# Moving the sums of the 32-wide score squares to TensorE, and more of the scores to GpSimd

## The chip, the cores and the metric

The kernel runs on one core of one Trainium2 chip. The metric is the device time of one execution in microseconds; lower is better. A core has five instruction streams that matter here: PE (TensorE; its weight loads are listed apart as PEld), DVE (VectorE), ACT (ScalarE), POOL (GpSimd) and SP, which issues DMAs. Each stream runs its own instructions in order and waits for the others through semaphores.

## The reference

The input x is (8, 512, 256): 8 batches of 512 tokens of width 256. Four blocks follow one another, each on a layer norm of x and each added to x: attention A, a feed-forward block, attention B, and the same feed-forward block again.

```python
# attention A: per token, the 64 channels of a head attend to one another
Q, K, V = (x @ W + b).reshape(b, s, 16, 64)            # Q scaled by 64**-0.5
scores = einsum('bshq,bshk->bshqk', Q, K)               # outer product, 64x64 per token and head
scores = where(triu(ones((64, 64)), 1), -inf, scores)   # causal in the channels
attn = einsum('bshqk,bshk->bshq', softmax(scores), V)
x = x + attn.reshape(b, s, 1024) @ Wo + bo
# feed-forward: 256 -> 1024 (gated, silu) -> 1024 (gelu) -> 1024 (gelu) -> 256, ternary weights
# attention B: the usual causal attention over 512 tokens, 16 heads of width 16
```

Attention A has no matrix product in its middle: for every token and head it needs a triangle of exp(q_i k_j), its row sums (the denominator), and its row sums weighted with v_j (the numerator).

## The kernel before

**Groups and units.** Attention A works on groups (batch b, four heads g, token tile i): 8 x 4 x 4 = 128 groups of 128 tokens by 256 channels. The triangle of a head is cut into squares below the diagonal: one of 32, two of 16, four of 8 and so on down to 1, and the diagonal itself. `units` splits a group into NU = 4 units: unit 0 holds the squares of 32 of two heads, unit 1 the squares of 16 of all four heads, unit 2 the squares of 32 of the other two heads, unit 3 all the smaller ones. Units 0 to 2 have 2048 score elements per token each, unit 3 has 1920. A tile `w` of 4096 columns holds the exponentials and, beside them, the exponentials times v.

**One unit's way.** `scores` multiplies q by k (POOL for units 0 and 2, DVE for units 1 and 3). `exps` takes the exponential on ACT. `weigh` multiplies by v on DVE. `halve` starts a DMA on POOL's queue that adds the second half of `w` to the first (units 0 to 2). For the squares of 32 `fold` then adds the halves of what is left on POOL. `gather` reduces the rest over the last axis on DVE into a small tile `red`, and `add_rows` adds that on POOL to `acc`, which holds denominator and numerator of the group. For unit 3 `gather` does the squares of 8 and 4, and `small_squares` those of 2 and 1 on POOL. When all units are in, `invert` (DVE) and `divide` (POOL) finish the group, `turn_group` transposes it on PE, and `project_out` multiplies it by Wo.

**The order.** It is written out by hand. `AttentionA.step(n)` issues the work of one step, one unit per step; `self.at(n - k)` is the unit that is k steps old, so the stages of different units overlap. A step has three parts, ended by `yield`. With u = n mod 4 for the unit that enters at step n, the parts always meet the same stages: `project` (q, k, v on PE) stands in part 2 of steps with n mod 4 = 1, `keep_qk` (ACT copies q and k out of PSUM) and `turn_group` in part 2 of n mod 4 = 2, `project_out` in part 2 of n mod 4 = 3, `new_x` in part 2 of n mod 4 = 0. After each part the main loop inserts slices of the rest (`after_a`: feed-forward, attention B, feed-forward of the previous batch), as much as a running total of estimated costs allows (`total = 309.5` per batch). So attention A of batch b runs beside the other three blocks of batch b - 1; batch 0 of attention A runs nearly alone, and so do the last three blocks of batch 7.

**Buffers.** The `w` tiles of units 0 and 2 rotate through three buffers; unit 1 has one of its own (`w16`). In PSUM there are two `qv` tiles (q and v of a group), five tiles `ps_f` for the other blocks, and `bank`, one tile of two halves of 256 columns; `half_bank` hands its halves out in turn to `project` (k), `turn_group`, `project_out` and the transpose of a layer norm of attention A.

Of the kernel before, what the change touches and what calls it, by code (L numbers as in the profile page):

```python
# [9 lines left out]
F32 = mybir.dt.float32  # L10
# [6 lines left out]
P = 128  # L17
# [267 lines left out]
def fast_path(ctx: ExitStack, tc: tile.TileContext, k, t, flag):  # L285
# [214 lines left out]


    bank = ps_a.tile([P, 2, GW], F32, name="bank")
    halves = [0]

    def half_bank():
        halves[0] ^= 1
        return bank[:, halves[0], :]

    def judge():

# [72 lines left out]

    JB = 8

    def pieces(w, n, off, nsq, cols):

        def of_rows(v):
            return v[:, cols].rearrange("p (x t) -> p x t", t=2 * n)[:, :, n:]

        def of_cols(v):
            return v[:, cols].rearrange("p (x t) -> p x t", t=2 * n)[:, :, :n]

        if n < 16:
            e, ev = (
                w[:, a * SMALL + off : a * SMALL + off + nsq * n * n].rearrange("p (x i j) -> p x i j", i=n, j=n)  # L600
                for a in range(2)
            )
            yield e, ev, lambda v: of_rows(v).unsqueeze(3), lambda v: of_cols(v).unsqueeze(2)
            return
        both = w.rearrange("p (b a x i j) -> p a b x i j", a=2, x=nsq, i=n, j=JB)
        if n == 32:
            for x in range(nsq):
                yield (
                    both[:, 0, :, x],
                    both[:, 1, :, x],  # L610
                    lambda v, x=x: of_rows(v)[:, x].unsqueeze(1).unsqueeze(3),
                    lambda v, x=x: of_cols(v)[:, x].rearrange("p (b j) -> p b j", j=JB).unsqueeze(2),
                )
        else:
            for k in range(n // JB):
                yield (
                    both[:, 0, k],
                    both[:, 1, k],
                    lambda v: of_rows(v).unsqueeze(3),
                    lambda v, k=k: of_cols(v)[:, :, k * JB : (k + 1) * JB].unsqueeze(2),  # L620
                )

    class AttentionA:
# [33 lines left out]
        def step(self, n):  # L657

            weighed = self.at(n - 2)
            if weighed[0] is not None:  # L660
                self.weigh(*weighed)
            unit = self.at(n)
            on_pool = unit[3] in (0, 2)
            if on_pool:
                half = self.scores(*unit)
                next(half)
            if weighed[0] is not None:
                self.halve(*weighed)
            if on_pool:
                next(half, None)  # L670
            b, i, g, u = self.at(n + 40)
            if u == 0 and g == 0 and i == 0 and b > 0:
                self.x[b] = load_x(b)
            b, i, g, u = self.at(n + 10)
            if u == 0 and g == 0 and i == 0 and b > 0:
                self.measure(b)
            b, i, g, u = self.at(n + 8)
            if u == 0 and g == 0:
                self.live["xn"] = normed(self.x[b][:, i, :], *self.rn[b, i], "a")
            b, i, g, u = self.at(n - 5)  # L680
            if u == NU - 1:
                self.invert(b, i, g)
            b, i, g, u = self.at(n - 4)
            if u == 1:
                self.gather(b, i, g, u)
            b, i, g, u = self.at(n + 7)
            if u == 0 and g == 0:
                nc.scalar.copy(self.live[b, i], self.live.pop("ps_ln"))
            if self.at(n - 1)[0] is not None:
                self.exps(*self.at(n - 1))  # L690
            yield
            if unit[0] is not None and not on_pool:
                for _ in self.scores(*unit):
                    pass
            for args in self.sums:
                self.add_rows(*args)
            self.sums = []
            b, i, g, u = self.at(n - 5)
            if u == NU - 1:
                self.divide(b, i, g)  # L700
            b, i, g, u = self.at(n - 2)
            if u == NU - 1:
                self.small_squares(b, i, g)

            b, i, g, u = self.at(n - 4)
            if u == 0:
                self.fold(b, i, g, u)
            b, i, g, u = self.at(n - 3)
            if u == 2:
                self.fold(b, i, g, u)  # L710
            b, i, g, u = self.at(n - 9)
            if u == NU - 1:
                self.new_x(b, i, g)
            b, i, g, u = self.at(n + 2)
            if u == 0:
                self.keep_qk(b, i, g)
            b, i, g, u = self.at(n - 7)
            if u == NU - 1:
                self.turn_group(b, i, g)
            b, i, g, u = self.at(n - 8)  # L720
            if u == NU - 1:
                self.project_out(b, i, g)
            b, i, g, u = self.at(n + 3)
            if u == 0:
                self.project(b, i, g)
            yield
            b, i, g, u = self.at(n - 4)
            if u == 2:
                self.gather(b, i, g, u)
            b, i, g, u = self.at(n - 5)  # L730
            if u == 0:
                self.gather(b, i, g, u)
            b, i, g, u = self.at(n - 3)
            if u == NU - 1:
                self.gather(b, i, g, u)
            b, i, g, u = self.at(n - 7)
            if u == NU - 1:
                nc.scalar.copy(self.live["att"], self.live.pop("pta"))
            b, i, g, u = self.at(n + 8)
            if u == 0 and g == 0:  # L740
                self.live[b, i] = lnp.tile([P, DC, P], F32, tag="xnt_a", name=f"xnta_{b}_{i}", bufs=NT)
                self.live["ps_ln"] = turned_over(self.live.pop("xn"), half_bank().rearrange("p (c s) -> p c s", c=DC))
            yield

        def measure(self, b, tiles=range(NT)):
# [39 lines left out]
        def scores(self, b, i, g, n_u):  # L785

            qv, kt = self.live[b, i, g][:2]
            if n_u == 0:
                acc = ap_.tile([P, 2, GW], F32, tag="acc", name=f"acc_{b}_{i}_{g}", bufs=3)
                self.live[b, i, g].append(acc)  # L790
                nc.vector.tensor_tensor(acc[:, 0, :], qv[:, 0], kt[:, 0], ALU.mult)

            if n_u in (0, 2):
                w = wt.tile([P, 4096], F32, tag="w", name=f"w_{b}_{i}_{g}_{n_u}", bufs=3)
            elif n_u == 1:
                w = wt.tile([P, 4096], F32, tag="w16", name=f"w16_{b}_{i}_{g}")
            else:
                w = wt.tile([P, 2 * SMALL], F32, tag="ws", name=f"ws_{b}_{i}_{g}")
            self.live[b, i, g, n_u] = w
            eng, q = (nc.gpsimd, kt[:, 1]) if n_u in (0, 2) else (nc.vector, qv[:, 0])  # L800
            for n, off, nsq, cols in squares(units[n_u]):
                for e, ev, rows, columns in pieces(w, n, off, nsq, cols):
                    shape = list(e.shape)
                    eng.tensor_tensor(  # L804
                        e, rows(q).to_broadcast(shape), columns(kt[:, 0]).to_broadcast(shape), ALU.mult
                    )
                    yield

        def exps(self, b, i, g, n_u):
            w = self.live[b, i, g, n_u]  # L810
            if n_u == 0:
                acc = self.live[b, i, g][2]
                nc.scalar.activation(acc[:, 0, :], acc[:, 0, :], AF.Exp, scale=C**-0.5)
            if n_u < NU - 1:
                e = w.rearrange("p (b a r) -> p a b r", a=2, b=units[n_u][0][0] // JB)[:, 0]
            else:
                e = w[:, :SMALL]
# [15 lines left out]
                w = self.live[b, i, g, n_u]  # L833
                nc.gpsimd.dma_start(w[:, :2048], w[:, 2048:], accum_op=ALU.add)  # L834

        def fold(self, b, i, g, n_u):

            w = self.live[b, i, g, n_u]
            nc.gpsimd.tensor_tensor(w[:, :1024], w[:, :1024], w[:, 1024:2048], ALU.add)  # L839

        def columns_of(self, w, n, off, nsq):

# [4 lines left out]

        def small_squares(self, b, i, g):

            w = self.live[b, i, g, NU - 1]  # L850
            for n, off, nsq, cols in squares(units[NU - 1]):
                if n <= 2:
                    both = self.columns_of(w, n, off, nsq)
# [4 lines left out]
        def gather(self, b, i, g, n_u):  # L858


            w = self.live.pop((b, i, g, n_u))
            for n, off, nsq, cols in squares(units[n_u]):
                if n > 2:
                    red = ap_.tile([P, 2, nsq * n], F32, tag=f"red{nsq * n}", name=f"red_{b}_{i}_{g}_{n_u}_{n}", bufs=2 + (n < 32))
                    nc.vector.tensor_reduce(red, self.columns_of(w, n, off, nsq), AX.X, ALU.add)  # L865
                    self.sums.append((b, i, g, n, cols, red))

# [158 lines left out]

    def fits(i, w, src):

        both = wt.tile([P, 2 * HB], F32, tag="w", name=f"w32_{i}", bufs=3)
        nc.sync.dma_start(both[:, :HB], src)  # L1030
        nc.vector.tensor_tensor(both[:, HB:], both[:, :HB], w, ALU.not_equal)
        nc.vector.tensor_reduce(unfit[:, i : i + 1], both[:, HB:], AX.X, ALU.max)
# [439 lines left out]
```

## Time and profile before

| | |
|---|---|
| Timed runs | 3984.17, 3989.1 and 3989.51 us; median 3989.1 us |
| Profiled execution, first to last instruction | span 3990.8 us; no other time is listed for it, and the span lies 0.04% above the median of the timed runs |
| Busy | PE 3039.9, PEld 2055.2, DVE 3375.9, ACT 2341.3, POOL 3077.9 us |
| Mean granted clock of TensorE | 0.849 |
| DMA queue on POOL (q0) | 570.46 MB, its packets took 63.2% of the 16 DMA engines' time |

"Busy" counts the time in which an engine executes an instruction; issuing DMAs and waiting on semaphores is not counted. A group line gives source line, engine, operation, output and inputs with their shapes, the count, then busy microseconds and the mean nanoseconds of one, then the idle time ahead of it and who ended it. `w<-w` DMA lines are the accumulating transfers of `halve`.

### The profile page before, as it was taken

Reading aid. Unit: us, or ns where it says so; the run is one execution under the profiler, and the core shown is the slowest. Engines: PE = TensorE matmul, PEld = TensorE weight load, DVE = VectorE, ACT = ScalarE, POOL = GpSimd, SP = SyncE. Lnnn points to the kernel's source line nnn. Section 1 sums busy time; section 2 is a strip of 40 time slices with the busy share of each in tenths; the row PEclk is TensorE's granted clock in tenths of the full one; section 3 lists DMA queues with packets and bytes.
Section 4 is the critical chain, followed back from the end, with each engine's and each line's share of the span. In section 5 each row is a group of like instructions: output and inputs, shape, how many; then the busy total and the mean of one; then the engine's idle time right before and its main releaser. Section 6 shows DMA issues by size and latency. Waiting matters only on the chain.

```text
span 3990.8 us, 37932 instructions
## 1 busy us (share of the span) xinstructions
PE 3039.9 (76%) x12464; PEld 2055.2 (52%) x12464; DVE 3375.9 (85%) x3776; ACT 2341.3 (59%) x3156; POOL 3077.9 (77%) x3040
## 2 busy tenths in 40 slices
PE   5653487687877878678876878778787778778988
PEld 2231264365634656356643656346553556446847
DVE  7999988998899888998899988998989888996115
ACT  3444475576665675666755766666755767565342
POOL 6888878887888788887788887887888877886111
PEclk7556599798987988888987989879898889879999
DMA  8766777577776877768775877668776677767304
GB/s 229 182 137 137 159 197 158 124 191 189 199 154 139 196 191 178 148 163 202 200 157 118 208 186 194 149 142 213 174 190 143 160 182 206 158 129 211 116 28 169
DMA packets 118346, 669.24 MB, mean 168 GB/s; under 512 B 12662, under 2 KB 31865, under 8 KB 43643
## 3 DMA queue, kind: packets, MB, share of 16 engines
q0 software_dynamic: 78336, 570.46, 63.2%
q1 hardware_dynamic: 39804, 96.27, 6.7%
q8 instruction: 101, 1.65, 0.2%
q14 instruction: 105, 0.86, 0.1%
HBM read 254.07 MB, written 9.96 MB: 66 GB/s over the span
## 4 chain that ended last, share of the span: by engine, by line
DVE 38%; PE 18%; POOL 14%; DMA 13%; ACT 8%; issue 8%; SPq 0%; ACTq 0%; POOLq 0%; DVEq 0%
DVE red L865 15%; DMA w<-w 13%; DVE w L828 10%; PE ph L1140 5%; ACT w L818 4%; POOL w L804 3%; POOL w L839 3%; DVE ws L828 3%; PE pqkb L1187 3%; POOL acc L872 3%; DVE w L804 2%; DVE ws L804 2%; POOL h L1056 2%; POOL w L834 2%; DVE acc L876 2%
## 5 line engine op out<-in xcount | busy, mean ns | idle before, releaser
L818 ACT ACTIVATE w<-w 128x2048 f32<-128x2048 f32 x384 | 733.8, 1912 | 659.2 <-POOL w L804 461.3
L1140 PE MATMUL ph<-h,hidden 128*128 128x512 f32 x4096 | 1042.9, 411 | 72.4 <-POOL h L1056 42.9
L804 POOL TENSOR_TENSOR w<-k 128x1024 f32<-128x1024 f32 x512 | 1077.4, 2104 | 7.7 <-ACT k L782 7.1
L1140 PEld LDWEIGHTS ph<-h,hidden 128*128 128x128 f32 x4096 | 792.3, 195 | 275.3 <-POOL h L1056 53.8
L828 DVE TENSOR_TENSOR w<-w,qv 128x1024 f32<-128x1024 f32 x768 | 898.8, 1211 | 22.4 <-ACT w L818 22.4
L865 DVE TENSOR_REDUCE red<-w 128x128 f32<-128x1024 f32 (+1 forms) x384 | 601.3, 1566 | 178.0 <-DMA w<-w 93.6
L839 POOL TENSOR_TENSOR w<-w 128x1024 f32<-128x1024 f32 x256 | 643.7, 2514 | 82.9 <-DMA w<-w 82.3
L834 POOL DMA_DIRECT2D w<-w x384 | 337.9, 880 | 349.0 <-issue 121.1
L872 POOL TENSOR_TENSOR acc<-acc,red 128x256 f32<-128x256 f32 (+1 forms) x640 | 471.2, 736 | 142.7 <-DVE red L865 122.0
L865 DVE TENSOR_REDUCE red<-ws 128x256 f32<-128x2048 f32 (+1 forms) x256 | 435.4, 1742 | 0.0
L766 PE MATMUL qv<-wqv,xnta 128*128 128x512 f32 x512 | 299.7, 716 | 104.6 <-DVE ws L828 95.4
L1072 PE MATMUL pw<-xnt,gate 128*128 128x512 f32 (+2 forms) x1152 | 301.8, 422 | 21.7 <-ACT silu L1048 16.1
L828 DVE TENSOR_TENSOR ws<-ws,qv 128x1024 f32<-128x1024 f32 (+3 forms) x512 | 294.3, 635 | 27.6 <-ACT ws L818 27.6
L804 DVE TENSOR_TENSOR w<-qv,k 128x1024 f32<-128x1024 f32 x256 | 301.1, 1218 | 3.6
L804 DVE TENSOR_TENSOR ws<-qv,k 128x1024 f32<-128x1024 f32 (+3 forms) x512 | 299.5, 646 | 0.2 <-issue 0.2
L888 PE MATMUL bank<-ident,acc 128*128 128x128 f32 x256 | 62.4, 333 | 284.5 <-ACT k L781 278.6
L818 ACT ACTIVATE ws<-ws 128x1920 f32<-128x1920 f32 x128 | 231.5, 1808 | 80.7 <-DVE ws L804 80.1
L1072 PEld LDWEIGHTS pw<-xnt,gate 128*128 128x128 f32 x1152 | 230.8, 215 | 76.2 <-ACT silu L1048 20.4
L1249 ACT ACTIVATE eb<-psb 128x256 f32<-128x256 f32 (+3 forms) x512 | 182.1, 443 | 139.1 <-PE psb L1246 138.6
L1166 PE MATMUL pof<-w,h 128*128 128x256 f32 x1024 | 244.9, 392 | 22.8 <-ACT h L1105 22.8
L1105 ACT ACTIVATE h<-ph,s_sb 128x512 fp32r<-128x512 f32 (+1 forms) x256 | 171.2, 688 | 151.1 <-PE ph L1140 149.7
L876 DVE RECIPROCAL acc<-acc 128x256 f32<-128x256 f32 x128 | 222.9, 1741 | 11.9 <-POOL acc L872 11.9
(149 smaller groups left out, 4846.4 us busy)
## 6 DMA issues: line engine op xcount, KB each, us to landing
w<-w POOLq DMA_DIRECT2D x384, 1024.0 KB, 7.8
hidden<-in_h POOLq DMA_DIRECT2D x128, 1024.0 KB, 7.9
gate<-in_w12p POOLq DMA_DIRECT2D x32, 1024.0 KB, 9.1
w<-w_d SPq DMA_DIRECT2D x16, 1024.0 KB, 11.5
wqv<-wqv_d SPq DMA_DIRECT2D x31, 512.0 KB, 4.6
wo<-in_wo SPq DMA_DIRECT2D x32, 256.0 KB, 7.6
wbqk<-wbqk_d SPq DMA_DIRECT2D x8, 1024.0 KB, 9.0
w<-in_h SPq DMA_DIRECT2D x8, 1024.0 KB, 8.6
```

The source lines that it names most:

```text
L766: nc.tensor.matmul(qv.rearrange("p j f -> p (j f)"), xnt[:, c, :], wqv[:, c, :], start=(c == 0), stop=(c == DC - 1),)
L804: eng.tensor_tensor(e, rows(q).to_broadcast(shape), columns(kt[:, 0]).to_broadcast(shape), ALU.mult)
L818: nc.scalar.activation(e, e, AF.Exp, scale=C**-0.5)
L828: nc.vector.tensor_tensor(ev, e, columns(qv[:, 1]).to_broadcast(list(e.shape)), ALU.mult)
L834: nc.gpsimd.dma_start(w[:, :2048], w[:, 2048:], accum_op=ALU.add)
L839: nc.gpsimd.tensor_tensor(w[:, :1024], w[:, :1024], w[:, 1024:2048], ALU.add)
L865: nc.vector.tensor_reduce(red, self.columns_of(w, n, off, nsq), AX.X, ALU.add)
L872: nc.gpsimd.tensor_tensor(rows, rows, part.rearrange("p a (x i) -> p a x i", i=n), ALU.add)
L876: nc.vector.reciprocal(acc[:, 0, :], acc[:, 0, :])
L1072: nc.tensor.matmul(pj[:, toks], w[:, m % 4, j, c, :], xs[:, p, c, toks], start=(p == 0 and c == 0), stop=(p == 1 and c == DC - 1),)
L1140: nc.tensor.matmul(pss[j], w[:, j, c, :], h_in(p, c), start=(p == 0 and c == 0), stop=(p == 1 and c == MC - 1),)
L1166: nc.tensor.matmul(po, h(0, c)[:, i * P : (i + 1) * P], w3[:, c, :], start=(c == 0), stop=False)
```

## The change

- The squares of 32 (units 0 and 2) get another layout in `w`: column j outermost, then exponential/weighted (a), square x and row i. After the halving DMA, 16 blocks of 128 columns are left that only have to be added up. `turn_sums` does it on PE: 16 transposes into the same 128 columns of PSUM, accumulating. `keep_sums` copies the result to SBUF on ACT, `turn_sums_back` transposes it back on PE, and `add_sums` adds it to `acc` on DVE. `fold`, the reductions and the `add_rows` of these units are gone.
- The scores of unit 1 (squares of 16) move from DVE to POOL.
- Units 0, 1 and 2 share one rotation of four buffers (`w16` goes).
- The half of `bank` with columns 256 to 511 now belongs to the sums; `half_bank` always returns the other.
- `small_squares` runs two steps later and in part 1 instead of part 2.
- Weighing of a unit of squares of 32 is one instruction of 2048 columns instead of two of 1024.

```diff
     def half_bank():
-        halves[0] ^= 1
-        return bank[:, halves[0], :]
+        return bank[:, 0, :]
...
-    def pieces(w, n, off, nsq, cols):
+    def pieces(w, n, off, nsq, cols, parts=1):
...
-        both = w.rearrange("p (b a x i j) -> p a b x i j", a=2, x=nsq, i=n, j=JB)
         if n == 32:
-            for x in range(nsq):
+            both = w.rearrange("p (j a x i) -> p a j x i", a=2, x=nsq, i=n)
+            step = n // parts
+            for k in range(0, n, step):
                 yield (
-                    both[:, 0, :, x],
-                    both[:, 1, :, x],
...
+                    both[:, 0, k : k + step],
+                    both[:, 1, k : k + step],
+                    lambda v: of_rows(v).unsqueeze(1),
+                    lambda v, k=k: of_cols(v)[:, :, k : k + step].rearrange("p x j -> p j x").unsqueeze(3),
                 )
...
@@ step, part 1
+            b, i, g, u = self.at(n - 4)
+            if u == NU - 1:
+                self.small_squares(b, i, g)
             unit = self.at(n)
-            on_pool = unit[3] in (0, 2)
+            on_pool = unit[3] in (0, 1, 2)
...
+            if self.at(n - 5)[3] in (0, 2):
+                self.keep_sums()
             if self.at(n - 1)[0] is not None:
                 self.exps(*self.at(n - 1))
             yield
@@ step, part 2
-            b, i, g, u = self.at(n - 2)
-            if u == NU - 1:
-                self.small_squares(b, i, g)
-
-            b, i, g, u = self.at(n - 4)
-            if u == 0:
-                self.fold(b, i, g, u)
-            b, i, g, u = self.at(n - 3)
-            if u == 2:
-                self.fold(b, i, g, u)
...
+            if self.at(n - 5)[3] in (0, 2):
+                self.turn_sums_back()
...
@@ step, part 3
-            b, i, g, u = self.at(n - 4)
-            if u == 2:
-                self.gather(b, i, g, u)
             b, i, g, u = self.at(n - 5)
-            if u == 0:
-                self.gather(b, i, g, u)
+            if u in (0, 2):
+                self.add_sums(b, i, g, u)
...
+            b, i, g, u = self.at(n - 4)
+            if u in (0, 2):
+                self.turn_sums(b, i, g, u)
             yield
...
@@ scores
-            if n_u in (0, 2):
-                w = wt.tile([P, 4096], F32, tag="w", name=f"w_{b}_{i}_{g}_{n_u}", bufs=3)
-            elif n_u == 1:
-                w = wt.tile([P, 4096], F32, tag="w16", name=f"w16_{b}_{i}_{g}")
+            if n_u < NU - 1:
+                w = wt.tile([P, 4096], F32, tag="w", name=f"w_{b}_{i}_{g}_{n_u}", bufs=4)
...
-            eng, q = (nc.gpsimd, kt[:, 1]) if n_u in (0, 2) else (nc.vector, qv[:, 0])
+            eng, q = (nc.gpsimd, kt[:, 1]) if n_u < NU - 1 else (nc.vector, qv[:, 0])
...
-        def fold(self, b, i, g, n_u):
-
-            w = self.live[b, i, g, n_u]
-            nc.gpsimd.tensor_tensor(w[:, :1024], w[:, :1024], w[:, 1024:2048], ALU.add)
+        def turn_sums(self, b, i, g, n_u):
+
+            w = self.live.pop((b, i, g, n_u))
+            for j in range(16):
+                nc.tensor.matmul(
+                    bank[:, 1, :P],
+                    w[:, j * P : (j + 1) * P],
+                    ident,
+                    start=(j == 0),
+                    stop=(j == 15),
+                    is_transpose=True,
+                )
+
+        def keep_sums(self):
+
+            self.live["sums"] = ap_.tile([P, P], F32, tag="sums", name="sums")
+            nc.scalar.copy(self.live["sums"], bank[:, 1, :P])
+
+        def turn_sums_back(self):
+
+            nc.tensor.transpose(bank[:, 1, P:], self.live.pop("sums"), ident)
+
+        def add_sums(self, b, i, g, n_u):
+
+            ((n, h0, nh),) = units[n_u]
+            acc = self.live[b, i, g][2]
+            rows = acc[:, :, h0 * C : (h0 + nh) * C].rearrange("p a (x t) -> p a x t", t=2 * n)[..., n:]
+            nc.vector.tensor_tensor(
+                rows, rows, bank[:, 1, P:].rearrange("p (a x i) -> p a x i", a=2, i=n), ALU.add
+            )
```

More of the change, by code (lines that the diff above doesn't have):

```diff
@@ L502, in fast_path @@
     bank = ps_a.tile([P, 2, GW], F32, name="bank")
-    halves = [0]
     def half_bank():
-        halves[0] ^= 1
-        return bank[:, halves[0], :]
+        return bank[:, 0, :]
     def judge():
@@ L604, in pieces @@
             return
-        both = w.rearrange("p (b a x i j) -> p a b x i j", a=2, x=nsq, i=n, j=JB)
         if n == 32:
-            for x in range(nsq):
+            both = w.rearrange("p (j a x i) -> p a j x i", a=2, x=nsq, i=n)
+            step = n // parts
+            for k in range(0, n, step):
                 yield (
-                    both[:, 0, :, x],
-                    both[:, 1, :, x],
-                    lambda v, x=x: of_rows(v)[:, x].unsqueeze(1).unsqueeze(3),
-                    lambda v, x=x: of_cols(v)[:, x].rearrange("p (b j) -> p b j", j=JB).unsqueeze(2),
+                    both[:, 0, k : k + step],
+                    both[:, 1, k : k + step],
+                    lambda v: of_rows(v).unsqueeze(1),
+                    lambda v, k=k: of_cols(v)[:, :, k : k + step].rearrange("p x j -> p j x").unsqueeze(3),
                 )
         else:
+            both = w.rearrange("p (b a x i j) -> p a b x i j", a=2, x=nsq, i=n, j=JB)
             for k in range(n // JB):
@@ L799, in scores @@
             self.live[b, i, g, n_u] = w
-            eng, q = (nc.gpsimd, kt[:, 1]) if n_u in (0, 2) else (nc.vector, qv[:, 0])
+            eng, q = (nc.gpsimd, kt[:, 1]) if n_u < NU - 1 else (nc.vector, qv[:, 0])
             for n, off, nsq, cols in squares(units[n_u]):
-                for e, ev, rows, columns in pieces(w, n, off, nsq, cols):
+                for e, ev, rows, columns in pieces(w, n, off, nsq, cols, parts=2):
                     shape = list(e.shape)
@@ L813, in exps @@
                 nc.scalar.activation(acc[:, 0, :], acc[:, 0, :], AF.Exp, scale=C**-0.5)
-            if n_u < NU - 1:
+            if n_u in (0, 2):
+                e = w.rearrange("p (j a r) -> p a j r", a=2, j=32)[:, 0]
+            elif n_u == 1:
                 e = w.rearrange("p (b a r) -> p a b r", a=2, b=units[n_u][0][0] // JB)[:, 0]
@@ L848, in small_squares @@
         def small_squares(self, b, i, g):
-            w = self.live[b, i, g, NU - 1]
+            w = self.live.pop((b, i, g, NU - 1))
             for n, off, nsq, cols in squares(units[NU - 1]):
@@ L858, in gather @@
         def gather(self, b, i, g, n_u):
-            w = self.live.pop((b, i, g, n_u))
+            w = self.live[b, i, g, n_u] if n_u == NU - 1 else self.live.pop((b, i, g, n_u))
             for n, off, nsq, cols in squares(units[n_u]):
                 if n > 2:
-                    red = ap_.tile([P, 2, nsq * n], F32, tag=f"red{nsq * n}", name=f"red_{b}_{i}_{g}_{n_u}_{n}", bufs=2 + (n < 32))
+                    red = ap_.tile([P, 2, nsq * n], F32, tag=f"red{nsq * n}", name=f"red_{b}_{i}_{g}_{n_u}_{n}", bufs=3)
                     nc.vector.tensor_reduce(red, self.columns_of(w, n, off, nsq), AX.X, ALU.add)
@@ L1027, in fits @@
     def fits(i, w, src):
-        both = wt.tile([P, 2 * HB], F32, tag="w", name=f"w32_{i}", bufs=3)
+        both = wt.tile([P, 2 * HB], F32, tag="w", name=f"w32_{i}", bufs=4)
         nc.sync.dma_start(both[:, :HB], src)
```

## The prediction

> **What bounds the kernel now.** I read the page's busy line first, then the group lines with shapes kept apart, then the table of windows, cut where one reciprocal (L876, one per group) starts: it shows groups 1 to 16 (batch 0, nearly alone), the next 111, and the rest after the last group's reciprocal.
>
> ```profile
> PE 3039.9 (76%) x12464; PEld 2055.2 (52%) x12464; DVE 3375.9 (85%) x3776; ACT 2341.3 (59%) x3156; POOL 3077.9 (77%) x3040
> ```
>
> ```profile
> core 0: us, PE busy (x) PEld busy (x) DVE busy (x) ACT busy (x) POOL busy (x), PEclk, DMA share, GB/s
> 0.00:458.55 458.55, 230.06 (x476) 115.67 (x477) 425.54 (x451) 186.28 (x202) 375.74 (x344) 0.60 0.73 167
> 458.55:3668.00 3209.45, 2511.14 (x10564) 1717.61 (x10564) 2864.81 (x3217) 2046.23 (x2738) 2650.15 (x2611) 0.87 0.73 173
> 3668.00:3990.80 322.80, 298.75 (x1427) 221.97 (x1425) 85.53 (x111) 108.81 (x217) 52.00 (x87) 0.97 0.32 113
> ```
>
> Three stages with different limits. In the **head** most groups take 23.7 us, and in the stretch 387.39 to 411.11 us DVE is busy for 23.68 of 23.71: DVE alone sets the pace. In the **middle** a group takes 3209.45/111 = 28.9 us, on average 25.8 busy on DVE, 23.9 on POOL, 22.6 on PE, 18.4 on ACT. No engine is full; groups beside attention B still take 23.7 to 26 us with DVE full, those beside the hidden layers 27 to 32 with PE busy up to 95%, those at a layer norm or gate 29 to 35 with none full. The **tail** is the last batch's other blocks, PE 93% busy; no group is in it.
>
> The waits say who is late in the middle:
>
> ```profile
> ACT w L818 <- POOL w L804: 461.3, 147, 7.5
> PE bank L888 <- ACT k L781: 278.6, 106, 5.8
> ...
> ACT w L818 <- DVE w L804: 164.2, 52, 8.4
> ```
>
> ACT's exponentials wait for scores, and PE, in `turn_group`, for ACT's copy of k, which stands behind an exponential. POOL and DVE are late first; ACT and PE pass it on.
>
> **What the Trainium skill says.** "TensorE: Matmul & The Clock Gate", "Part 4: PE-mode transpose": about 275 ns for a 128x128 transpose inside a kernel, and the full clock isn't earned by transposes. The trace's shortest (L1312) takes 272 ns, the median 421; whether a burst lets the clock fall no row here shows. The same page, "LDWEIGHTS (loading the stationary operand)", prices a load at columns/1.2, an estimated 107 ns for 128: the spacing in a burst, if matmul and load overlap. The trace agrees:
>
> ```profile
> 760.03 0.57 PEld L1312 LDWEIGHTS pytb<-ident,ytb 128*128 128x128 f32 x4
> 760.24 0.60 PE L1312 MATMUL pytb<-ident,ytb 128*128 128x128 f32 x4
> ```
>
> Four take 0.60 us, the last of them 0.27, so each follows the one before by (0.60-0.27)/3 = 0.11 us at full clock. In the head (clock 0.57) two (L567) take 0.69 us, one 0.42: 0.27 us apart. "Trainium Kernel Development and Optimization", "Key Constraints": GpSimd cannot access PSUM. So the last addition must go to DVE; no POOL row here reads a PSUM tile.
>
> **The change part by part**, per group (128 groups), with these rows:
>
> ```profile
> L804 POOL TENSOR_TENSOR w<-k 128x1024 f32<-128x1024 f32 x512 | 1077.4, 2104 | 7.7 <-ACT k L782 7.1
> L839 POOL TENSOR_TENSOR w<-w 128x1024 f32<-128x1024 f32 x256 | 643.7, 2514 | 82.9 <-DMA w<-w 82.3
> L865 DVE TENSOR_REDUCE red<-w 128x128 f32<-128x1024 f32 x256 | 309.5, 1209 | 84.2 <-POOL w L839 84.1
> L804 DVE TENSOR_TENSOR w<-qv,k 128x1024 f32<-128x1024 f32 x256 | 301.1, 1218 | 3.6
> L872 POOL TENSOR_TENSOR acc<-acc,red 128x128 f32<-128x128 f32 x256 | 179.6, 702 | 0.3 <-DVE red L865 0.3
> ```
>
> - *POOL.* Out: two folds (2 x 2.51) and two `add_rows` (2 x 0.70). In: two score instructions (2 x 2.10; 1.9 to 2.5 for the changed patterns, by the L804 and L839 rows). Net -2.2 us, bounds -2.6 to -1.4. The three `halve` issues (0.88 each) stay.
> - *DVE.* Out: two score instructions (2 x 1.22), two reductions (2 x 1.21). In: two `add_sums` of 128 columns from PSUM (0.28 each, the 128x128 product's row; 0.42, the 256-column PSUM row, at most). One weighing of 2048 for two of 1024: 2.28 (the 2048-column reduction) against 2.42, twice, -0.3 (0 at least). Net -4.6, bounds -4.9 to -4.0.
> - *ACT.* In: two copies out of PSUM, 0.28 each (the 128x128 exponential from PSUM): +0.6.
> - *PE.* In: 32 transposes in two bursts, two back. Full clock: 2 x (15 x 0.11 + 0.27) + 2 x 0.27 = 4.4 us. Clock of the head: 2 x (15 x 0.27 + 0.42) + 2 x 0.42 = 9.8. Middle, clock 0.87: between; nearer the low end, since the clock is low mostly where PE idles. I take 5.
> - *Moved:* `small_squares` (one 0.70 and two 0.80 on POOL, no DMA) goes past one `halve` issue and four score instructions on POOL, to the one step in four that now has no scores there. It still stands before `invert`. POOL's and DVE's work per step becomes even. No DMA is added and SP's queue is untouched; the weight loads on POOL now stand behind unit 1's scores too, 4.2 us later at most; they are issued two weight tiles ahead, which covers that unless PE runs short of POOL's pace. `turn_sums` stands two and two thirds of a step after its `halve`, 19 us at 7.2 us a step, against 0.9 to issue and 7.8 to land: no wait. The fold's wait for it (82.3 us in all) goes; the reduction of unit 1, two steps after its own, keeps its wait (93.6 us in all).
> - *Buffers.* Unit 1 takes at step n+1 of the next group the buffer that unit 0 held: POOL's score waits for PE's burst at the end of the step just before. Behind it on POOL stand the halving DMAs and weight loads, and ACT's next exponential waits for it. Other reuses have a step or more of slack.
> - *New PE/ACT hand-overs.* `bank` is one tile, and in the built order the bursts wait for ACT: after `new_x` in one step, after `att` in another; ACT's `keep_sums` waits for the burst with the next exponentials queued behind; `turn_sums_back` waits for ACT, with `project` or `project_out` behind; DVE's `add_sums` waits for PE, with the next weighing behind. Each has about a third of a step (2.4 us) of slack, which other blocks fill. Unseen before; bounds 0 and 3 us a group (the L888 wait, of the same kind with no slack, costs 278.6/128 = 2.2). No gain lies in a wait as such. I take 0.5.
>
> Now the stages. **Head:** DVE would allow 23.7-4.6 = 19.1. But at the low clock PE and ACT form a ring through `bank`, with the timeline's durations: bursts 2 x 4.5, back 2 x 0.4, `project` 2.1+3.4, `turn_group` 0.7, `project_out` 2.9, ACT's five copies between them 1.6: 20.5. I add an estimated 1.5 for exponentials in the way of those copies (one takes 1.9): 22. Against 23.7 that is -1.7 for 16 groups: **-30**, bounds -70 (DVE's limit) and +20 (a stall of 1.3 more than it gains).
>
> **Middle:** PE 22.6+5 = 27.6, DVE 25.8-4.6 = 21.2, POOL 23.9-2.2 = 21.7 plus its issues, ACT 19.0. PE becomes the fullest engine, and a group can't be shorter than its share. Groups beside hidden layers (a little over a third) already have PE at 23 to 28: they end near 30.5, about 1 longer. Gate and layer-norm groups (a third) lose part of the lateness of POOL and DVE: -1.7 of 32.5. Groups beside attention B (under a third) go from 25.3 to about 23.7, -1.6. Weighted: 0.37 x 1 - 0.32 x 1.7 - 0.31 x 1.6 = -0.7, and with denser work a slightly better clock, -0.8: 111 x -0.8 = **-90**. **Tail:** no change.
>
> Sum: 3990.8-30-90 = **3870 us**. The span stands 0.04% over the median of the runs, so it is taken as the time.
>
> **The rivals.**
> - *A, the forecast* (0.56): 3870, itself 3770 to 3970. For: DVE full in the head and beside attention B, and every late engine but PE is relieved.
> - *B, the clock follows* (0.11): waits for POOL and DVE vanish, PE runs nearly without gaps at full clock. PE's middle at clock 1 is about 2511 x 0.9 + 111 x 4.4 = 2750; at 95% use 2890, so -320 there and -40 in the head: 3630. Against: hidden layers already run at 0.95 to 1.0.
> - *C, gain and loss cancel* (0.05): 3983 to 3997.
> - *D, slower* (0.28): PE becomes the bound, in the middle's `bank` ring. If a transpose costs 0.2 us (the clock falls in bursts) and the hand-overs 1.5 us, PE has 22.6+8+1.5 = 32.1 us a group: 111 x 3.2 = +355, a third of it hidden in groups where PE idles more, less 30 in the head: 4200. It decides where the added PE time with its waits passes 28.9-22.6 = 6.3 us a group. For: the L888 wait, and PE at 95% in hidden groups. Against: the 0.11 us spacing.
>
> **How the numbers follow.** Likeliest: 3870. The range reaches down a third short of B on the way from A, 3710, and up to most of the way to D, 4110; what it leaves out is the far side of each. Two tenths of one per cent (8 us) is about what a measurement can tell here. Faster is A, less 0.01 for its upper edge, and B: 0.66; same is C: 0.05; slower is D and that edge: 0.29. A's own range stands above, 3770 to 3970.
>
> **What would show it.** Right: bursts of 16 in about 2 us beside feed-forward, PE's busy share over 85% and above DVE's; DVE near 2790, POOL near 2800, ACT near 2410 us; the waits of ACT for POOL's scores halved; head groups near 22 us. Wrong: bursts of 3 us and more, clock under 0.85, long waits of ACT for PE in `keep_sums` or of PE for ACT in the bursts, or POOL waiting for PE at unit 1's scores; then D. A tail that isn't near 323 us would be outside all of this.

## The result and the profile after

The changed kernel takes 4013.86 us (median of 4 runs, 4007.79 to 4019.47) against 3989.31 for the kernel before: ratio 1.006, 95% interval 1.0048 to 1.0072. It is slower by 25 us where the prediction said faster by 120. The profiled execution spans 4012.2 us at a mean granted clock of 0.911 (before: 0.849).

The page's busy line of the changed kernel, and its table of windows, cut as before at the 17th and the last reciprocal of a group (now L899):

```profile
PE 3367.7 (84%) x16816; PEld 2501.8 (62%) x16816; DVE 2849.4 (71%) x3264; ACT 2389.0 (60%) x3412; POOL 2886.4 (72%) x2784
```

```profile
core 0: us, PE busy (x) PEld busy (x) DVE busy (x) ACT busy (x) POOL busy (x), PEclk, DMA share, GB/s
0.00:429.40 429.40, 274.08 (x1058) 192.06 (x1059) 352.24 (x378) 192.12 (x236) 355.36 (x312) 0.76 0.79 179
429.40:3687.10 3257.70, 2795.17 (x14326) 2088.73 (x14325) 2411.85 (x2777) 2087.12 (x2959) 2479.42 (x2386) 0.92 0.73 171
3687.10:4012.20 325.10, 298.43 (x1435) 221.05 (x1434) 85.36 (x111) 109.77 (x218) 51.60 (x86) 0.97 0.31 106
```

DVE has lost 526 us of work and GpSimd 191, PE gained 328. The head shrank by 29 us, the tail is 2 us longer, and the middle **grew** by 48 us (3257.7 against 3209.45), although DVE is busy for only 74% of it and no engine for more than 86%. Work went away and waiting took its place. The list of waits, longest in total first (who waited for whom: us in total, times, longest), with other lines left out (`...`):

```profile
ACT sums L849 <- PE bank L837: 459.0, 171, 5.3
POOL w L831 <- DVE w L825: 424.1, 217, 6.8
...
DVE acc L860 <- POOL acc L895: 220.4, 114, 7.4
...
PE bank L911 <- ACT k L778: 179.3, 77, 4.5
DVE acc L860 <- PE bank L491: 174.4, 52, 9.7
...
POOL w L799 <- PE bank L837: 134.2, 67, 5.4
PE bank L837 <- ACT x L930: 124.2, 47, 6.8
...
ACT w L815 <- POOL w L799: 74.7, 56, 3.5
```

ACT's exponentials no longer wait for scores (74.7 us against 461.3). Instead ACT waits for the burst (`keep_sums`), the burst for ACT's copy of x, GpSimd's scores for the burst, and DVE's `add_sums` for GpSimd's `add_rows` and for PE. The second line of the list, 424.1 us, is GpSimd's `halve` waiting for DVE's weighing, which stands behind `add_sums`: GpSimd and DVE take turns as well. Here is a knot between PE and ACT in the timeline of the changed kernel, beside attention B, first PE, then ACT (start, us taken, instruction, and in brackets the idle time before it and who ended it):

```profile
2054.94 3.67 PE L837 MATMUL bank<-ident,w 128*128 128x128 f32 x16 [3.94 <-ACT x L930]
2058.54 1.94 PE L1277 MATMUL pyb<-eb,vb 128*32 128x512 f32 x8
2060.41 0.96 PE L1265 MATMUL psb<-qkb,qkb 32*128 32x384 f32 x8
2061.30 0.40 PE L1269 MATMUL psb<-tmask,ident 128*128 128x128 bf16 x4
2063.47 0.33 PE L853 MATMUL bank<-ident,sums 128*128 128x128 f32 x1 [1.78 <-ACT sums L849]
```

```profile
2050.87 2.06 ACT L1272 ACTIVATE eb<-psb 128x512 f32<-128x512 f32 x4 [0.86 <-PE psb L1269]
2052.80 1.82 ACT L815 ACTIVATE ws<-ws 128x1920 f32<-128x1920 f32 x1
2054.49 0.39 ACT L930 COPY x<-bank 128x256 f32<-128x256 f32 x1
2061.62 1.64 ACT L1272 ACTIVATE eb<-psb 128x384 f32<-128x384 f32 x4 [6.74 <-PE psb L1269]
2063.12 0.30 ACT L849 COPY sums<-bank 128x128 f32<-128x128 f32 x1
```

PE stands still for 3.94 us because the copy of x is behind 3.9 us of exponentials on ACT; in that idle time the granted clock drops (0.85 over these 4 us, 0.50 in the burst), so the burst takes 3.67 us; attention B's next scores stand behind the burst, so ACT then idles 6.74 us waiting for them; `keep_sums`, whose data were ready at 2058.6, stands behind attention B's exponentials in turn and keeps PE waiting another 1.78 us. Neither engine is short of time; each waits for the other in turn. The slow burst is no exception: in the middle, the 123 bursts with less than 0.2 us of idle time before them take 1.99 us on average at a clock of 0.98, the 13 that follow 3 to 4 us of idle time 3.48 us at 0.54.

### The profile page after: what moved, and what is told of

Read it like the earlier page. It is cut to its first block, busy times and chain, and to the rows that moved or that the text cites. A ratio compares the mean times of both kernels' runs of the same rounds, so it can differ in the third digit from the quotient of the medians.

```text
span 4012.2 us, 46672 instructions
## 1 busy us (share of the span) xinstructions
PE 3367.7 (84%) x16816; PEld 2501.8 (62%) x16816; DVE 2849.4 (71%) x3264; ACT 2389.0 (60%) x3412; POOL 2886.4 (72%) x2784
## 4 chain that ended last, share of the span: by engine, by line
PE 53%; ACT 17%; POOL 12%; DVE 10%; issue 5%; DMA 2%; ACTq 0%; POOLq 0%; DVEq 0%; SPq 0%
PE ph L1163 15%; PE bank L837 11%; POOL w L799 5%; ACT w L815 5%; PE pof L1189 4%; DVE w L825 4%; PE pw L1095 3%; PE qv L763 3%; PE pqkb L1210 3%; PE pyb L1277 3%; ACT eb L1272 2%; POOL acc L895 2%; PE psb L1265 2%; DVE red L888 2%; ACT L815 2%
## 5 line engine op out<-in xcount | busy, mean ns | idle before, releaser
L799 POOL TENSOR_TENSOR w<-k 128x1024 f32<-128x1024 f32 x768 | 1607.5, 2120 | 161.4 <-PE bank L837 134.2
L1163 PE MATMUL ph<-h,hidden 128*128 128x512 f32 x4096 | 1014.2, 401 | 23.3 <-POOL h L1079 22.0
L825 DVE TENSOR_TENSOR w<-w,qv 128x2048 f32<-128x2048 f32 (+1 forms) x512 | 883.7, 1747 | 15.0 <-ACT w L815 14.1
L1163 PEld LDWEIGHTS ph<-h,hidden 128*128 128x128 f32 x4096 | 762.6, 189 | 198.9 <-POOL h L1079 25.5
L815 ACT ACTIVATE w<-w 128x2048 f32<-128x2048 f32 x384 | 734.4, 1915 | 77.0 <-POOL w L799 74.7
L837 PE MATMUL bank<-ident,w 128*128 128x128 f32 x4096 | 620.4, 316 | 184.9 <-ACT x L930 124.2
L831 POOL DMA_DIRECT2D w<-w x384 | 340.4, 887 | 561.8 <-DVE w L825 424.1
L837 PEld LDWEIGHTS bank<-ident,w 128*128 128x128 f32 x4096 | 566.0, 165 | 242.1 <-ACT x L930 138.1
L860 DVE TENSOR_TENSOR acc<-acc,bank 128x128 f32<-128x128 f32 x256 | 73.4, 287 | 557.5 <-POOL acc L895 220.4
L849 ACT COPY sums<-bank 128x128 f32<-128x128 f32 x256 | 69.2, 270 | 459.0 <-PE bank L837 459.0
L895 POOL TENSOR_TENSOR acc<-acc,red 128x256 f32<-128x256 f32 x384 | 323.2, 842 | 22.4 <-DVE red L888 12.0
L888 DVE TENSOR_REDUCE red<-w 128x256 f32<-128x2048 f32 x128 | 291.8, 2280 | 32.5 <-DMA w<-w 32.5
L825 DVE TENSOR_TENSOR ws<-ws,qv 128x1024 f32<-128x1024 f32 (+3 forms) x512 | 295.3, 639 | 26.1 <-ACT ws L815 25.7
L763 PE MATMUL qv<-wqv,xnta 128*128 128x512 f32 x512 | 254.6, 622 | 3.4 <-DVE ws L825 1.6
```

Source lines behind the costliest of these rows:

```text
L763: nc.tensor.matmul(qv.rearrange("p j f -> p (j f)"), xnt[:, c, :], wqv[:, c, :], start=(c == 0), stop=(c == DC - 1),)
L799: eng.tensor_tensor(e, rows(q).to_broadcast(shape), columns(kt[:, 0]).to_broadcast(shape), ALU.mult)
L815: nc.scalar.activation(e, e, AF.Exp, scale=C**-0.5)
L825: nc.vector.tensor_tensor(ev, e, columns(qv[:, 1]).to_broadcast(list(e.shape)), ALU.mult)
L837: nc.tensor.matmul(bank[:, 1, :P], w[:, j * P : (j + 1) * P], ident, start=(j == 0), stop=(j == 15), is_transpose=True,)
L895: nc.gpsimd.tensor_tensor(rows, rows, part.rearrange("p a (x i) -> p a x i", i=n), ALU.add)
```

## The experiments

Three theories. **R:** hand-overs through `bank` between PE and ACT (and on to DVE and GpSimd) set the middle. **O:** PE's added time does. **P:** unit 1's scores on GpSimd, waiting for PE's burst, do. Every kernel below starts from the changed one unless it says otherwise. Ratios are to the kernel before on the same chip. Its median was 3985.5 to 3990.0 us on the chips used, so a difference in microseconds between kernels measured on two chips is uncertain by some 5 us more than the intervals say. The diffs are cut to what matters, and a line of words in them stands for the calls that it names.

**Copies of x and k ahead of the exponentials** (`e1_early`). Part 1 of a step, on ACT:

```diff
             if self.at(n - 5)[3] in (0, 2):
                 self.keep_sums()
+            new_x and keep_qk, from part 2
             if self.at(n - 1)[0] is not None:
                 self.exps(*self.at(n - 1))
```

> Only ACT's order changes: new_x and keep_qk move from part 2 to part 1, ahead of the exponentials, so that PE's burst and turn_group find their copies made earlier. Theory R (the middle is set by hand-overs between PE and ACT through `bank`, worst beside attention B, where the copies stand behind exponentials): 3900 to 3960 us, the groups beside attention B fall from about 29 towards 26 us, and PE's waits for the copies of x and k (124 and 179 us) fall below half. Theory O (it is PE's added time as such, 620 us of bursts): within 15 us of the changed kernel's 4014. Theory P (unit 1's scores on GpSimd wait for PE's burst and hold everything up): within 15 us of 4014 as well.

Measured: 3930.28 us, ratio 0.9864 (0.9848 to 0.9881). An order of ACT alone, with no work changed, is worth 84 us: R's range. PE's waits for the two copies fell below half, as R had it (124.2 to 50.0 and 179.3 to 66.5 us), while that for `att` grew from 51.5 to 136.2. O and P fail here as full explanations.

**One transpose per burst** (`e2_one`): `range(16)` becomes `range(1)` in `turn_sums`.

> Each burst makes 1 of its 16 transposes; the other 15 are left out (so most of the squares of 32 is missing from the sums). All hand-overs stay, 3840 transposes go, at least 3840 x 0.11 = 420 us of PE. Theory R: only the groups where ring and burst coincide gain, 3850 to 3920 us. Theory O: the gain shows in nearly every group of the middle, 3650 to 3750 us. Theory P: like O in so far as the burst's end comes earlier, 3750 to 3850.

Measured: 3811.35 us, ratio 0.9561 (0.9545 to 0.9577): 203 us less than the changed kernel, between the ranges of R and O and inside P's. So PE's time does count, but it isn't all. The mean granted clock falls as well, from 0.911 to 0.855, so the 203 us are what the missing transposes gave less what the lower clock took.

**No path of sums at all** (`e4_nosums`): the calls of `turn_sums`, `keep_sums`, `turn_sums_back` and `add_sums` go.

> The whole path of the sums of 32 is left out (turn_sums, keep_sums, turn_sums_back, add_sums; these squares are missing from the result). What is left is the relief of DVE and GpSimd alone. Theory R: at least 80 us faster than the kernel with one transpose per burst, since the hand-overs are gone too. Theory O: within 40 us of it. In either case far below the kernel before, 3600 to 3750 us, if DVE and GpSimd bounded that one as the prediction had it.

Measured: 3614.69 us, ratio 0.9073 (0.9057 to 0.9088). That is 197 us below the kernel with one transpose: over 80, as R had it, not within 40, as O did. The relief of DVE and GpSimd alone was worth 375 us; the path of sums cost 399: 203 for 15 of 16 transposes and 197 for what is left, hand-overs with the few short instructions in them (one transpose there and one back, a copy, an addition per burst).

**Unit 1's scores back on DVE** (`e3_dve16`): `on_pool` and the engine chosen in `scores` for units 0 and 2 only.

> One part undone: the scores of unit 1 go back to DVE; buffers and the path through TensorE stay as changed. Theory P: 3930 to 3980 us, since GpSimd no longer waits for the burst ahead of the halving DMAs. Theories R and O: 4000 to 4060 us, DVE has 2.4 us a group more and nothing on the PE/ACT ring has changed.

Measured: 4048.15 us, ratio 1.0152 (1.0135 to 1.0169), 34 us slower than the changed kernel. P falls: moving these scores to GpSimd was a gain. The scores' wait for the burst all but went with the move (134.2 us on GpSimd, 8.0 on DVE), and the kernel still got slower.

**Copy of att early as well** (`e5_att`): on top of the early copies of x and k, ACT's copy of `att` goes from part 3 to directly behind `turn_group` in part 2.

> As the kernel with the early copies (3930 us), and ACT's copy of att follows turn_group in part 2 at once, ahead of other blocks' work on ACT, so that the burst of unit 2 finds it made (PE waits 136 us for it there). Theory R (hand-overs through `bank` set the middle): 3870 to 3915. Theory O (what is left is PE's added time): 3920 to 3940.

Measured: 3893.0 us, ratio 0.9753 (0.9732 to 0.9774); 37 us less, in R's range.

**`keep_sums` behind the exponentials** (`e6_keep`), on top of the early copies of x and k:

```diff
-            keep_sums ahead of exps
             if self.at(n - 1)[0] is not None:
                 self.exps(*self.at(n - 1))
+            keep_sums
...
+            turn_sums_back at the end of part 2
```

> As the kernel with the early copies, and keep_sums stands behind the exponentials instead of ahead of them (turn_sums_back moves to the end of part 2). ACT then doesn't hold exponentials back while it waits for PE's burst (377 us of waits in keep_sums). If the direction PE to ACT of the ring costs: 3870 to 3915. If only the direction ACT to PE does: 3925 to 3960, since turn_sums_back and the addition then come later.

Measured: 4107.75 us, ratio 1.0295 (1.0278 to 1.0312): 177 us slower than without this edit, outside both ranges. Its list of waits is now led by

```profile
DVE acc L860 <- PE bank L853: 593.5, 158, 10.5
ACT eb L1272 <- PE psb L1269: 268.5, 97, 7.4
ACT k L778 <- DVE acc L860: 265.1, 75, 6.2
PEld bank L758 <- ACT sums L849: 215.3, 89, 7.2
```

A later copy makes the transposition back late, DVE stands in `add_sums` with the next weighing behind it, and ACT's copy of k then waits for DVE. Letting the exponentials go first does not make the hand-over cheaper here. Two things were moved, the copy and the transposition back, and which of them costs more wasn't taken apart.

**Control: early copies in the kernel before** (`e7_before_early`), the same two moves there.

> Control: the same early copies of x and k in the kernel before. Theory R says that the early copies helped because the changed kernel made PE's bursts wait for them; here only turn_group waits (279 us in all) and DVE and GpSimd set the pace: 3960 to 3990. If the copies' place was a fault of both kernels alike: about 84 us here too, 3905.

Measured: 3979.84 us, ratio 0.9974 (0.9966 to 0.9982). 10 us here against 84 in the changed kernel: the place of these copies became dear through the change.

**DVE folds first, half the transposes** (`e8_fold`), on top of the early copies of x and k; part 1 of the burst's step, on DVE, and 8 transposes instead of 16:

```diff
+            if u in (0, 2):
+                w = self.live[b, i, g, u]
+                nc.vector.tensor_tensor(w[:, :1024], w[:, :1024], w[:, 1024:2048], ALU.add)
```

> As the kernel with the early copies, but DVE adds the halves of what is left of a unit of 32 first (1024 columns, 1.2 us, twice a group), in part 1 of the burst's step, and a burst makes 8 transposes instead of 16. Theory O (PE's time): 15 of 16 transposes less gave 203 us, so 8 of 16 give about 105 before DVE's 2.4 us a group, which DVE can take (it is busy 22 of 29 us): 3830 to 3880. Theory R: the hand-overs stay and the burst also waits for DVE: 3910 to 3960.

Measured: 4278.18 us, ratio 1.0728 (1.071 to 1.0746): 348 us slower than with 16 transposes, far from both ranges. The group of the new addition and of the burst:

```profile
L691 DVE TENSOR_TENSOR w<-w 128x1024 f32<-128x1024 f32 x256 | 578.6, 2260 | 25.9 <-DMA w<-w 25.9
L840 PE MATMUL bank<-ident,w 128*128 128x128 f32 x2048 | 372.8, 342 | 682.9 <-issue 357.8 <-DVE w L691 207.3 <-ACT att L735 104.0
```

The addition takes 2.26 us in the mean, not 1.2, and PE idles 683 us ahead of bursts that are half as long; at least 207 of these are waits for DVE, and of 358 the profile names no cause. PE's busy work fell and the time rose: another hand-over, in front of the burst, costs more than the transposes it saves. Why the addition is long is taken up at the end of this text. How much of the loss is the long addition and how much its place wasn't taken apart.

**`add_rows` behind `add_sums`** (`e9_rows`), on top of all three early copies: the loop over `self.sums` goes from part 2 to behind `add_sums` in part 3.

> As the kernel with early copies of x, k and att (3893 us), and the add_rows of the reductions stand on GpSimd behind add_sums, at the end of part 3, instead of ahead of it in part 2. DVE's add_sums then waits less for GpSimd (234 us in all before it). If that wait is one of the hand-overs that cost: 3860 to 3885. If DVE has slack there, as its 22 of 29 us a group say: 3885 to 3905; slower than that if invert then waits for the later add_rows.

Measured: 3825.43 us, ratio 0.9601 (0.9582 to 0.962), 68 us less, below the range. DVE stopped waiting for GpSimd in `add_sums` (233.7 us before this move, 2.0 after), and GpSimd's `halve` for the weighing behind it (344.4 to 36.5); what is left is one wait the other way round. The first line of its list of waits:

```profile
POOL acc L893 <- DVE acc L858: 408.1, 184, 6.2
```

**Burst of unit 0 a part earlier** (`e10_burst2`), on top of the three early copies, with `add_rows` where it was:

> As the kernel with early copies of x, k and att (3893 us), and the burst of unit 0 stands in part 2 instead of part 3, so that GpSimd's scores into the same buffer (they wait 104 us for the burst) and ACT's keep_sums (321 us) find it done earlier. Theory R (hand-overs cost, in both directions): 3850 to 3885. Theory O (what is left is PE's added time): 3885 to 3900. Slower, over 3905, if the burst then waits longer for ACT's copy of x.

Measured: 3867.38 us, ratio 0.97 (0.9683 to 0.9716); 26 us less, in R's range.

**All four moves** (`e11_all`).

> All four moves together: early copies of x, k and att, add_rows behind add_sums, burst of unit 0 in part 2. If the hand-overs cost one by one, the gains of the last two (68 and 26 us on 3893) add: about 3800. If they loosen the same wait: 3820 to 3830.

Measured: 3820.2 us, ratio 0.9582 (0.9562 to 0.9602), level with the kernel without the earlier burst. That is the range for two moves that loosen the same wait. This version beats both kernels: 170 us below the kernel before and 194 below the changed one, with the same instructions on every engine as the latter.

**All four moves, one transpose per burst** (`e12_all_one`).

> The same with 1 of 16 transposes per burst (the sums of 32 are incomplete), to see what PE's time is worth once the hand-overs are loose. In the changed kernel the 15 transposes were worth 203 us (4014 to 3811). Theory O, PE's time by itself: again about 200 below the kernel with all four moves, 3600 to 3640. Theory R, much of that was the burst's length inside the PE/ACT ring: a smaller difference, 60 to 140 us.

Measured: 3665.16 us, ratio 0.9185 (0.917 to 0.9201): 155 us below the kernel with all four moves, between the two ranges. Of the 203 us that the transposes cost in the changed kernel about 50 went with the looser ring; some 155 stay.

Where in a batch the time lies shows when the intervals between the reciprocals of successive groups are taken from the timeline and averaged by place in the batch (groups 33 to 112, five batches): four places beside attention B's scores and values, and the other twelve.

| us per group | beside attention B | elsewhere |
|---|---|---|
| before | 25.0 | 30.3 |
| changed | 28.0 | 29.8 |
| early copies of x, k | 26.0 | 29.5 |
| all four moves | 25.1 | 28.8 |
| one transpose | 26.3 | 28.0 |
| no path of sums | 21.5 | 27.4 |

Beside attention B the burst's transposes cost 1.7 us a group (28.0 to 26.3) and what remains of the path 4.8 (26.3 to 21.5); elsewhere 1.8 and 0.6. In the middle, the hand-overs are dear where ACT has long exponentials and PE's scores feed it. In the head, too, they cost 2.3 us a group (22.3 to 20.0), and the transposes nothing (22.3 with 16 and with one).

## Why the prediction was wrong, point by point

- **What bounds the kernel before: right.** With the path of sums left out, the relief of DVE and GpSimd gave 375 us.
- **The head: right in the number, by luck.** Its groups take 22.3 us (predicted 22), the head 29 us less (predicted 30). But the forecast put a ring of PE and ACT there, in which the two bursts are 9 of 20.5 us. The head doesn't follow the bursts' length (22.3 us a group with one transpose as well) nor the copies' place (22.4 with x and k early); with `add_rows` behind `add_sums` it falls to 21.3, without the path of sums to 20.0. So part of it is the turn-taking of GpSimd and DVE, which the forecast didn't have. First GpSimd, then DVE in the changed kernel's head:

```profile
319.02 4.14 POOL L799 TENSOR_TENSOR w<-k 128x1024 f32<-128x1024 f32 x2
322.85 1.00 POOL L895 TENSOR_TENSOR acc<-acc,red 128x256 f32<-128x256 f32 x1
323.54 2.23 POOL L799 TENSOR_TENSOR w<-k 128x1024 f32<-128x1024 f32 x1
327.00 0.88 POOL L831 DMA_DIRECT2D w<-w  x1 [1.23 <-DVE w L825]
```

```profile
323.88 0.29 DVE L860 TENSOR_TENSOR acc<-acc,bank 128x128 f32<-128x128 f32 x1 [2.00 <-POOL acc L895]
324.08 0.42 DVE L822 TENSOR_TENSOR acc<-acc,qv 128x256 f32<-128x256 f32 x1
324.42 2.28 DVE L825 TENSOR_TENSOR w<-w,qv 128x2048 f32<-128x2048 f32 x1
```

  `add_sums` (L860) waits for `add_rows` (L895), which stands behind two score instructions; the weighing (L825) follows, and `halve` (L831) waits for it. **The tail:** 325 us, as good as unchanged.
- **The prices of the instructions: within the bounds, if not always near.** DVE 2849 us (predicted near 2790), GpSimd 2886 (2800), ACT 2389 (2410). GpSimd's relief is 191/128 = 1.5 us a group, where 2.2 was forecast with 1.4 as the least. These are the rows for the burst, GpSimd's scores of all three units, the weighing in one piece and the addition from PSUM in the changed kernel:

```profile
L837 PE MATMUL bank<-ident,w 128*128 128x128 f32 x4096 | 620.4, 316 | 184.9 <-ACT x L930 124.2 <-ACT att L732 51.5 <-DMA w<-w 8.8
L799 POOL TENSOR_TENSOR w<-k 128x1024 f32<-128x1024 f32 x768 | 1607.5, 2120 | 161.4 <-PE bank L837 134.2 <-issue 12.2 <-DVE red L888 7.3
L825 DVE TENSOR_TENSOR w<-w,qv 128x2048 f32<-128x2048 f32 x256 | 583.9, 2281 | 5.3 <-ACT w L815 4.4
L860 DVE TENSOR_TENSOR acc<-acc,bank 128x128 f32<-128x128 f32 x256 | 73.4, 287 | 557.5 <-POOL acc L895 220.4
```

  The burst is 620.4/128 = 4.8 us a group, the two transposes back are another 0.6; 5 was taken. A burst at full clock takes 1.91 us (15 x 0.11 + 0.27 = 1.92 was worked out):

```profile
1968.27 1.91 PE L837 MATMUL bank<-ident,w 128*128 128x128 f32 x16
```

  So the spacing in a burst, 0.11 us, is what the section "LDWEIGHTS (loading the stationary operand)" of "TensorE: Matmul & The Clock Gate" in the Trainium skill gives for loading 128 columns, for accumulating transposes too. The same page's section "Part 4: PE-mode transpose" says that the full clock isn't engaged by transposes. For these fp32 transposes the runs say otherwise: in the head, where attention A runs nearly alone, the granted clock is 0.76 with 16 transposes per burst (0.60 before), and with one of 16 it is 0.61, in a head of almost the same length:

```profile
0.00:426.80 426.80, 241.05 (x545) 122.60 (x546) 352.32 (x378) 194.62 (x237) 354.57 (x312) 0.61 0.79 180
```

- **The hand-overs: wrong, and this is the step that failed.** They were counted at 0.5 us a group, a term that the sum of the middle does not name, on the ground that each had a third of a step of slack "which other blocks fill". From one transpose per burst to none they measure 197/128 = 1.5 us a group, with the few short instructions in them, the very number that rival D had put in. And they don't spread: beside attention B they are 4.8 us. There other blocks don't fill the slack: PE and ACT already take turns in a chain (scores, exponentials, values), so a wait put into it holds up both, as in the knot above, and the idle time lowers the clock of the burst that follows. The early copies of x and k gave 2.0 us a group there and 0.3 elsewhere. Of the forecast's signs of being wrong, the long waits came (459.0 us in `keep_sums`, 124.2 of the bursts for x, 134.2 of GpSimd's scores for the burst); the low clock did not.
- **The middle's weighting: wrong by the same step.** The groups beside attention B were to gain 1.6 us and lost 3.0: the relief alone was 3.5 there (25.0 to 21.5), and the path took 6.5. Elsewhere 0.5 us was gained, not far from what the two other terms gave together (0.37 x 1 - 0.32 x 1.7, spread over 0.69 of the groups: -0.25), but neither term came out by itself: the six places with most of the hidden layers' matmuls went from 28.9 to 27.9 us (forecast: about 1 longer), the other six from 31.7 to 31.9 (forecast: 1.7 shorter).
- **The chain from GpSimd to DVE wasn't seen.** "DVE's `add_sums` waits for PE" was named; that it also waits for GpSimd's `add_rows` on the same `acc`, which now stands behind two more score instructions, was not. Turning that order round was worth 68 us, 10 of them in the head; of the moves tried, only the early copies of x and k gave more.
- **Rival D** had the mechanism, and its hand-overs were right; a transpose at 0.2 us was too dear (0.15 in the mean, 620.4/4096), and in the middle 15 of 16 of them cost only 1.7 to 1.8 us a group of the time. The measured 4014 lies near neither it nor the forecast, but inside the range.

What stays open: whether giving the sums a bank of their own would have freed them of the copies of x, k and att altogether. It wasn't tried. Nor were the shared rotation of four buffers, the new place of `small_squares` and the weighing in one piece undone one by one, so their shares aren't known.

## What to carry to other kernels

When work moves to an engine with idle time, ask what that idle time is: beside attention B PE was idle because it was taking turns with ACT, and a burst put there lengthened the turn. Price a new hand-over by what stands ahead of it in the queue of the engine that must answer, stage by stage, not by an average slack; then put the answer early in that queue, ahead of long instructions. Four such moves of order, with no instruction added or dropped, turned 0.6% slower into 4.2% faster.

## What was not expected of the hardware

- DVE's addition of two full 1024-column fp32 operands of one tile took 2.26 us in the mean over 256 (1.16 to 5.24 in the answer for its line), where the product of 1024 with a broadcast operand takes 1.21. The view of the line:

```profile
L691 DVE TENSOR_TENSOR w<-w x256: 1161/2354/5241, 37.6 to 3941.5; 128x1024 f32<-128x1024 f32 x128
```

  It isn't a fixed price, and the trace shows what goes with the long ones: the 108 additions that started while GpSimd was idle all took 1.22 us, the 133 that started while GpSimd was in a score instruction 2.98 us in the mean (1.47 to 5.24). The weighing of 2048 columns, whose second operand lies in PSUM, takes 2.28 us in the mean in the same run, whether it started beside a GpSimd instruction (192 of 256) or not. This is read from one trace; no run changes GpSimd's part alone.
- More work on PE cost less than its sum: the bursts are 620 us busy and the transposes back 79, but PE's total rose by 328. At a mean clock of 0.911 instead of 0.849 its other matmuls took less time: the 512 for q and v 254.6 us against 299.7, the 4096 of the hidden layers 1014.2 against 1042.9, and smaller ones likewise. The transposes themselves raised that clock: leaving out 15 of 16 brought it back to 0.855.
